# A projection by seven half-size products in place of eight, with its buffers in one ring, in a two-layer graph attention kernel on one Trainium2 core

## The chip, the core and the metric

The kernel runs on one core of a Trainium2 chip. The core has four compute engines with an instruction queue each: TensorE multiplies 128x128 blocks into PSUM, VectorE and ScalarE work elementwise on SBUF and PSUM, GpSimd does elementwise work and the indexed DMAs. SyncE issues most of the other DMAs. An instruction waits, on its engine, until what it needs is there; everything behind it on that engine waits too.

The metric is the time of one execution on the device, in microseconds, lower is better. In the profile PE is TensorE's multiplying, PEld its loading of weights, DVE is VectorE, ACT ScalarE, POOL GpSimd, SP SyncE. "L762" is line 762 of the kernel before.

## What is computed

The input is x, 16 batches of 1024 nodes with 256 features in float32, and one adjacency matrix of 1024 x 1024. Two layers follow each other, each with a layer norm ahead and x added behind:

```python
def _gat(inp, adj_mask, W, a):
    h = jnp.matmul(inp, W)
    F_ = h.shape[-1]
    f1 = jnp.matmul(h, a[:F_, 0])
    f2 = jnp.matmul(h, a[F_:, 0])
    e = jax.nn.leaky_relu(f1[:, :, None] + f2[:, None, :], ALPHA)
    if adj_mask is not None:
        e = jnp.where(adj_mask[None, :, :] > 0, e, NEG_INF)
    att = jax.nn.softmax(e, axis=2)
    h_prime = jnp.einsum('bij,bjf->bif', att, h)
    return jax.nn.elu(h_prime)

def _L0_gnn_ref(x, adj, mlp1_w, mlp1_b, mlp2_w, mlp2_b, W_fc, a_fc, W_hand, a_hand):
    out = jax.nn.relu(jnp.matmul(x, mlp1_w) + mlp1_b)          # 256 -> 512
    residual = out
    out = _gat(jax.nn.relu(out), None, W_fc, a_fc)             # first attention, no mask
    out = jax.nn.elu(out) + residual
    out = jax.nn.relu(jnp.matmul(out, mlp2_w) + mlp2_b)        # 512 -> 256
    residual = out
    out = _gat(jax.nn.relu(out), adj, W_hand, a_hand)          # masked attention a
    out = jax.nn.elu(out) + residual
    return jax.nn.relu(out)

h = jnp.maximum(_layernorm(x, axis=-1), 0.0)
x = x + _L0_gnn_ref(h, adj, ...)
h = jnp.maximum(_layernorm(x, axis=-1), 0.0)
x = x + _L1_gnn_ref(h, adj, L1_gnn_W, L1_gnn_a)                # masked attention b
```

The change is about `h = inp · W_fc` of the first, unmasked attention: 1024 x 512 times 512 x 512 in each of the 16 batches.

## The kernel before

**Stages of one batch.** Layer norm and a transpose; `mlp1` (L748) writes `resT`, 128 partitions x 4 chunks x 1024 nodes (features on the partitions). `project` (L762) multiplies `resT` by `wfc_sb`: for each of 8 tiles of 128 nodes and each of two column halves g, four chunks of 128 features are added up in PSUM. A half has 257 columns; the last one is f1 (half 0) or f2 (half 1), since the weights carry the products with the attention vector. ScalarE copies each half (L764) into `h_nat`, and GpSimd takes f1 out and puts ones in its place (L766, L767).

**The unmasked attention has no products of 1024 x 1024.** Since its weights depend on f1 + f2 alone, the nodes are sorted by f2, prefix sums of the sorted rows are written as tables, and each node gathers two rows. The steps: `columns` and `send` lay out f2 as a row, `rank` (L808 to L815) counts on VectorE how many nodes stand ahead, `scatter` (L822) writes the rows of `h_nat` to memory in sorted order, `read_sorted` (L866) loads them into `xs`, `sum_before` and `sum_behind` (L894 to L909) form sums into `tt` and `xs`, `write_table` and `carry` write the tables `fine` and `coarse`, `gather` (L934) fetches rows of them into `got`, `share` (L946 to L949) forms the denominators, `mean` (L956, L959) the mean rows, and `merge` (L1006 to L1017) transposes them, applies elu and adds the residual in `resT`. For the first batch half of this is done by products instead.

**Then** `mlp2` (L1024), the projection of the masked attention a (L614), its weights on VectorE (L667) and products (L677), `finish`, `combine` and `update` (L689 to L710), the second layer norm, and the same for the masked attention b (L717 to L723).

**Order.** All of it is written out by hand. `at(name, lo, hi, steps)` gives each step a planned time, to which the table `SHIFT` adds a number; all steps are sorted by that time, and every engine has its instructions in that order. GpSimd's instructions are also chained to each other. A period of the plan is 142 units (134.15 us in the trace between two like bursts), and a batch's work is spread over several periods: the rows of batch b + 2 are projected, ranked and scattered in the period in which batch b is in the masked attentions, and the prefix sums and gathers of batch b + 1 lie between. The planned places of the projection:

```python
for t in range(NT):
    at("dense_rows1", t0 + BETWEEN[t], t0 + BETWEEN[t], [partial(dense[b].project, t, 1)])
...
at("dense_begin5", t0 - 33, t0 - 30.5, [partial(d.project, t, 0) for t in range(2)])
at("dense_begin6", t0 - 21, t0 - 8, [partial(d.project, t, 0) for t in range(2, NT)])
```

**Buffers.** Each tag is a ring: an allocation takes the next buffer of the tag, and its first writer waits for the last reader of what was there. `seq` has two full-size buffers, which `h_nat`, `xs`, `tt` and `got` take in turn; `hm` has two of half that size for the projected rows of the masked attentions; `att` has eight of 128 x 256 for the masked weights.

Of the kernel before, what the change touches and what calls it, by code (L numbers as in the profile page):

```python
# [17 lines left out]
P = 128  # L18
HALF = 512
# [9 lines left out]
D_MIN = 1.0e-7  # L29
SHIFT = {  # L30
    "end dense_begin1": (-2.54,),
    "end dense_begin2": (-0.99,),
    "end dense_begin4": (9.79, 10.84, 0, 0, 0, -3.05, 0, -5.96,),
    "end dense_begin5": (-23.89, -15.67,),
    "end dense_begin6": (-20.81, 0, -12.64, -10.02, -11.47, -12.26,),
    "end dense_begin7": (-3.07,),
    "end dense_end1": (-7.17, -1.95,),
    "end dense_end2": (-6.38, -6.38, -6.38, -6.38,),
    "end dense_rows1": (-10.51, -6.24, -6.82, 0, 0, 0, 0, -4.24,),
    "end dense_sums1": (-48.96,),  # L40
    "end dense_sums10": (-21.95,),
    "end dense_sums2": (8.53, 0, 0, 3.76, -8.53, -12.13, -7.88, -5.24,),
    "end dense_sums3": (-9.59, -12.4,),
    "end dense_sums4": (-7.91, -7.91, -7.91, -7.91, -3.45, -3.45, -3.45, -3.45,),
    "end dense_sums6": (10.61,),
    "end dense_sums7": (-3.22, -4.43, -3.58, -3.26, 0, -0.77, 0, 4.02,),
    "end dense_sums8": (3.76,),
    "end dense_sums9": (2.37,),
    "end early_gathers2": (10.03, 10.03,),
    "end early_gathers3": (-5.29, 18.84, 14.56, 18.48,),  # L50
    "end early_gathers4": (0, 0.45, 0, 0, 10.2, 15.36, 8.86, 10.63,),
    "end first_mlp1": (-7.09, 0, 0, -10.32,),
    "end first_mlp2": (-4.41, -4.41, -4.41, -4.41,),
    "end masked_first1": (-9.1,),
    "end masked_first10": (0, 0.7, -4.33, -3.67, -2.03, -1.81, -3.41,),
    "end masked_first11": (0, 0, -4.93, -4.17, -2.96, -1.43, -4.36, -0.47,),
    "end masked_first12": (0, -1.5,),
    "end masked_first13": (0, 0, -4.74, -4.15, 0, 0.69, 1.51, 0.6,),
    "end masked_first14": (0.61, 3.4, -2.77, -2.71, 0.32, 3.65, 1.3, 0.83,),
    "end masked_first15": (-2.98,),  # L60
    "end masked_first16": (0.15,),
    "end masked_first2": (-8.7,),
    "end masked_first4": (-7.99,),
    "end masked_first5": (-9.93, -3.59, -1.25,),
    "end masked_first7": (-18.06, 0, 3.52, 24.98,),
    "end masked_first9": (-2.7, -2.7, -2.7, -2.7, -2.7, -2.7, -2.7, -2.7, -1.13, -0.9, -1.12,
        -1.51, -1.92, -2.78, -3.21, -3.56, -4.22, -2.23, -1.85, -1.53, -1.76, -2.17, -2.28, -2.05,
        -5.73, -5.67, -4.93, -4.1, -4.46, -4.69, -5.08, -4.71, -7.38, -5.64, -6.02, -5.94, -4.67,
        -3.38, -2.99,),
    "end masked_second1": (0, 0, 0, 0, 0, 0, -2.7, -2.7, -2.7, -2.7, -2.7, -2.7, -4.75, -4.45, 0,  # L70
        0, 0, 0, 0, 1.61, 1.54, 3.47, 3.07, 3.3, -3.32, -2.79, 0, 0, 0, 0.67, -6.09, -6.45, -6.84,
        -3.49, 0, 2.45,),
    "end masked_second2": (0, 0, 0, 0, 0, 0, 3.2, 2.96, 0.23, 0.23, 0, 2.22,),
    "end masked_second3": (-0.67, -0.43, 0, 0, -0.54, 3.58, 2.58, 1.28,),
    "end masked_second4": (0, 0, 0, 0, 0, 2.18, 2.56, 4.8,),
    "end masked_second5": (14.49, 8.09, 12.75, 21.36, 24.19, 12.45,),
    "end masked_second6": (0, 17.47,),
    "end merges1": (-2.65, -5.36, -2.83, -5.06, 0, 2.68, 2.67, 0.66,),
    "end merges2": (-2.65, -5.24, 5.1, 1.49, 3.05, 1.93, 4.16, 11.78,),
    "end scatters1": (8.25, 10.06, -7.13, -3.44, -5.23, -10.63, 0, -8.12,),  # L80
    "end second_mlp1": (1.82, 4.66, 8.88, 11.17,),
    "end second_mlp2": (-9.26, -9.26, -9.26, -9.26, -9.26, -9.26, -9.26, -9.26,),
    "end second_mlp3": (-9.24,),
    "end second_norm1": (-4.45, -1.81, -4.63, -4.57, -4.39, -5.31, -5.93, -6.31,),
    "end second_norm2": (-6.82,),
    "end second_norm3": (-6.84,),
    "end second_norm4": (-7.95,),
    "end second_norm5": (-8.56, -3.63, -2.16, -3.25, -3.33, -6.23, -7.8,),
    "end second_norm6": (-7.46,),
    "end second_norm8": (0, 0, 0, 0, 31.85,),  # L90
    "end turn_at1": (-3.4, 0, 0, -4.89, -0.78, -0.78, -0.78, -0.78,),
    "end turn_at2": (0, 0, 0, 0.78, -1.37, -1.37, -1.37, -1.37,),
    "end weights a": (-5.34, -5.34, -5.34, -5.34, -5.34, -5.34, -5.34, -5.34, -1.3, -1.76, -8.73,
        -6.94, -1.68, -8.23, 0, 1, 0.15, 0, 0, 0, -7.3, 1.55, 0, 0, -2.46, -12.74, -3.66, -1.38,
        -1.88, -1.72, -2.61, -5.89, -4.74, -29.97, -2.33, -12.21, -4.28, -4.33, -3.77, -7.66,),
    "end weights b": (-7.6, -7.02, -8.62, -8.6, -3.43, -3.15, -2.16, 1.28, -7.9, -5.17, -3.12,
        1.84, 1.74, 2.72, -12.96, -7.11, -4.91, -8.89, -1.88, -2.69, -5.62, -3.89, -12.92, 1.63,
# [1759 lines left out]
```

## Time and profile before

| what | value |
|---|---|
| time, median of 3 runs | 2252.36 us (2252.07 to 2253.29) |
| the profiled execution's own time | 2251.37 us |
| its span in the profile | 2249.6 us |
| PE busy | 2207.2 us, 98% of the span |
| DVE busy | 1643.1 us, 73% |
| ACT busy | 1259.6 us, 56% |
| POOL busy | 954.4 us, 42% |
| moved by DMA | 368.95 MB, 164 GB/s in the mean |

The span runs from the first to the last instruction; the execution's time has 1.8 us more. A group's row of the profile has the line, the engine, the operation, what it writes and reads, shapes and type, the count, then busy time, the mean length of one, and the idle time of the engine just ahead of them with what ended it. Lengths of PE rows overlap: the sum of their rows may exceed PE's busy time. A wait's row has who waited for whom, the sum, the count and the longest.

### The profile page before, as it was taken

To read this page: it belongs to the slowest core of one execution; us is meant where nothing else is said; L and a number is where in the kernel's file an instruction comes from. 1 tells how busy PE (TensorE), PEld (TensorE's weight loads), DVE (VectorE), ACT (ScalarE), POOL (GpSimd) and SP (SyncE) were. 2 spreads that over 40 slices of the span, in tenths; PEclk is the share of its full clock that TensorE was granted. 3 is DMA by queue.
4 is the path that set the end of the run, shared out by engine and by line. 5 is a ranking of instruction groups with operands and counts; after the bars stand their busy time and mean duration, and the time that the engine had idled before them with its cause. 6 is when DMAs were issued, how large, how long until landed. Compare 5 with 4: busy or idle time off the path is not lost.

```text
span 2249.6 us, 31025 instructions
## 1 busy us (share of the span) xinstructions
PE 2207.2 (98%) x9754; PEld 1723.4 (77%) x9754; DVE 1643.1 (73%) x4535; ACT 1259.6 (56%) x2797; POOL 954.4 (42%) x1212
## 2 busy tenths in 40 slices
PE   7999999999999999999999999999999999999997
PEld 5767777787877878787787877878787787877776
DVE  7677676777867678776776867677786776858765
ACT  5355745547365564756557375564746557365542
POOL 1163425263452536425263452636435263543620
PEclk9999999999999999999999999999999999999999
DMA  5568466675766757566685666757566585645700
GB/s 197 159 175 196 114 208 154 186 183 148 197 123 200 187 168 190 137 196 148 192 191 147 189 127 194 188 177 189 130 205 144 185 197 153 164 125 169 178 22 28
DMA packets 263870, 368.95 MB, mean 164 GB/s; under 512 B 124352, under 2 KB 175880, under 8 KB 259600
## 3 DMA queue, kind: packets, MB, share of 16 engines
q1 hardware_dynamic: 217088, 202.72, 31.9%
q0 software_dynamic: 45952, 163.99, 28.9%
q8 instruction: 80, 1.31, 0.3%
q14 instruction: 94, 0.77, 0.1%
q10 hardware_dynamic: 656, 0.17, 0.0%
HBM read 226.88 MB, written 126.29 MB: 157 GB/s over the span
## 4 chain that ended last, share of the span: by engine, by line
PE 75%; DVE 6%; DMA 2%; POOL 2%; ACT 1%; issue 1%; POOLq 0%; DVEq 0%; ACTq 0%; SPq 0%
PE oa L677 17%; PE h L762 16%; PE ob L677 14%; PE m L1024 8%; PE m L748 6%; PE pa L614 4%; PE pb L614 3%; PE hpT L1006 2%; DMA got<-coarse,k 2%; DVE attb L667 1%; PE carry L918 1%; PE on L1038 1%; PE nt L536 1%; DVE stats L516 1%; DVE hp L959 1%
## 5 line engine op out<-in xcount | busy, mean ns | idle before, releaser
L677 PE MATMUL ob<-hmb,attb 128*128 128x257 f32 x2048 | 463.9, 380 | 2.2 <-DVE attb L667 1.9
L762 PE MATMUL h<-wfc_sb,resT 128*128 128x257 f32 x2048 | 462.8, 379 | 0.0
L677 PE MATMUL oa<-hma,atta 128*128 128x258 f32 x2048 | 459.9, 382 | 1.8 <-DVE atta L667 1.5
L677 PEld LDWEIGHTS ob<-hmb,attb 128*128 128x128 f32 x2048 | 383.9, 190 | 67.2 <-issue 12.3
L677 PEld LDWEIGHTS oa<-hma,atta 128*128 128x128 f32 x2048 | 384.8, 190 | 59.3 <-DVE atta L667 2.9
L762 PEld LDWEIGHTS h<-wfc_sb,resT 128*128 128x128 f32 x2048 | 380.1, 189 | 59.1 <-issue 7.4
L705 POOL TENSOR_TENSOR posa<-posa,onat 128x256 f32<-128x256 f32 x118 | 106.7, 904 | 546.1 <-ACT posa L693 487.6
L667 DVE SCALAR_TENSOR_TENSOR attb<-rowsb,qwdb,edge 128x256 f32<-128x256 f32 (+1 forms) x536 | 292.1, 563 | 34.6 <-PE ob L677 28.6
L667 DVE SCALAR_TENSOR_TENSOR atta<-rowsa,qwda,edge 128x256 f32<-128x256 f32 (+1 forms) x520 | 257.3, 524 | 51.4 <-DMA rowsa<-row_a 35.6
L934 POOL DMA_INDIRECT got<-coarse,k x124 | 203.4, 1640 | 90.9 <-DMA got<-fine,k 56.6
L748 PE MATMUL m<-hT,w_sb 128*128 128x512 f32 x512 | 236.6, 596 | 1.9 <-ACT rb L719 1.1
L1024 PE MATMUL m<-resT,w_sb 128*128 128x512 f32 x512 | 228.3, 593 | 1.0 <-POOL resT L1017 1.0
L719 ACT ACTIVATE rb<-ob,recb 128x256 f32<-128x256 f32 x128 | 58.5, 474 | 274.9 <-DVE recb L717 248.9
L1017 POOL TENSOR_TENSOR resT<-resT,e 128x512 f32<-128x512 f32 x128 | 165.5, 1295 | 104.9 <-DVE e L1016 96.7
L692 ACT ACTIVATE ea<-oa,reca 128x256 f32<-128x256 f32 x128 | 60.3, 471 | 248.1 <-DVE reca L689 228.7
L934 POOL DMA_INDIRECT got<-fine,k x124 | 126.7, 1022 | 128.5 <-DVE hpd L999 41.9
L1024 PEld LDWEIGHTS m<-resT,w_sb 128*128 128x128 f32 x512 | 94.5, 190 | 102.4 <-issue 93.5
L748 PEld LDWEIGHTS m<-hT,w_sb 128*128 128x128 f32 x512 | 94.2, 191 | 89.0 <-issue 74.7
L822 POOL DMA_INDIRECT sorted<-hnat,place x128 | 128.6, 1004 | 53.9 <-DVE place L815 33.0
L764 ACT COPY hnat<-h 128x257 f32<-128x257 f32 x256 | 90.8, 367 | 104.1 <-PE h L762 101.6
L845 ACT ACTIVATE junk<-r,fs 128x1024 int8<-128x1024 f32 x124 | 142.6, 1150 | 0.9 <-POOL fs L766 0.6
L1016 DVE SCALAR_TENSOR_TENSOR e<-hpT,e 128x512 f32<-128x512 f32 x128 | 87.9, 688 | 53.2 <-ACT e L1010 53.0
(195 smaller groups left out, 3391.2 us busy)
## 6 DMA issues: line engine op xcount, KB each, us to landing
xs<-sorted SPq DMA_DIRECT2D x32, 1028.0 KB
fine<-tt SPq DMA_DIRECT2D x32, 1026.0 KB
fine<-xs SPq DMA_DIRECT2D x32, 1026.0 KB
x<-in_x_dram SPq DMA_DIRECT2D x16, 1024.0 KB
xn<-in_x_dram SPq DMA_DIRECT2D x15, 1024.0 KB
out_dram<-x SPq DMA_DIRECT2D x28, 512.0 KB
hT<-xn SPq DMA_DIRECT2D x416, 32.0 KB
coarse<-carry SPq DMA_DIRECT2D x32, 256.5 KB
```

The costliest lines, as they stand in the source:

```text
L614: nc.tensor.matmul(ps[:, :2 + F], lhsT=hT[:, c, t * P:(t + 1) * P], rhs=self.w_sb[:, c, 0, :], start=(c == 0), stop=(c == FC - 1))
L667: nc.vector.scalar_tensor_tensor(a_t[:, :n * P], self.rows[:, i], self.qwd[:, 1, j:j + 1], edge[:, j, i], op0=OP.max, op1=OP.mult)
L677: nc.tensor.matmul(self.out[t][:, :F + self.ONES], lhsT=self.att[t0, j][:, (t - t0) * P:(t - t0 + 1) * P], rhs=self.hm[:, j, 2:2 + F + sel ...
L705: adder.tensor_add(pos, pos, o_nat[:, t, :])
L748: nc.tensor.matmul(ps, lhsT=w1_sb[:, kc, c * P:(c + 1) * P], rhs=piece(kc, h), start=(kc == 0), stop=(kc == FC - 1))
L762: nc.tensor.matmul(ps[:, :F + 1], lhsT=self.resT[:, kc, t * P:(t + 1) * P], rhs=wfc_sb[:, kc, g, :], start=(kc == 0), stop=(kc == HC - 1))
L764: nc.scalar.copy(self.h_nat[:, t, g, :], ps[:, :F + 1])
L822: made = nc.gpsimd.indirect_dma_start(out=sorted_d[self.b % 2], out_offset=bass.IndirectOffsetOnAxis(ap=self.place[:, t:t + 1], axis=0), i ...
L845: nc.scalar.activation(junk, self.r2, AF.Sign, bias=self.fs[:, 0, t:t + 1], accum_out=self.signs[:, t:t + 1])
L934: nc.gpsimd.indirect_dma_start(out=got[u // n][:, u % n, :], out_offset=None, in_=(coarse_d if coarse else fine_d)[self.b % 2][:, :], in_o ...
L1017: nc.gpsimd.tensor_add(dst, dst, e)
L1024: nc.tensor.matmul(ps, lhsT=w2_sb[:, kc, c * P:(c + 1) * P], rhs=self.resT[:, kc, h * HALF:(h + 1) * HALF], start=(kc == 0), stop=(kc == H ...
```

## The change

**The projection.** `resT` is cut in 2 x 2 blocks (upper and lower 512 nodes; first and last two chunks of features), and so is the weight (chunks by column halves g). Seven products by the scheme of Strassen and Winograd give the four blocks of h. For each pair u of node tiles (u and u + 4) the products 1, 6, 5 and 3 add up in one PSUM bank, and after each of them ScalarE copies the running sum out as one of the four blocks; product 7 of two pairs goes to another PSUM buffer and VectorE adds it to two blocks (`add_pair`); products 2 and 4 are separate and are added by VectorE to the blocks that hold f1. A product has two chunks of 128 features.

**The sums.** Each pair needs four sums of blocks of `resT`, two on VectorE and two on GpSimd (`sums_of`). Four sums of weight blocks are formed once, on GpSimd (`seven_weights`). The weight block that is overwritten there is first stored to memory, and read from there in each batch (`load_b21`, two DMAs of 128 x 257).

**Buffers.** `seq` and `hm` become one ring of six half-size buffers: `h_nat`, `xs` and `tt` take two each, `got` four of two tiles, the two masked projections one each. The sums and the re-read weight block take buffers of the ring `att`, which are widened to 257 columns. Some small tiles move to other tags or have fewer buffers. `share` works on pairs of tiles.

**The places.** The steps of the sort, the scatter and the prefix sums have new planned times, `send` of the masked attention b is placed by the next batch's period, the start is rearranged, and the whole table `SHIFT` is new.

```diff
+SEQ = 6
 SHIFT = {
...
-        a_bc = big.tile([P, 2, fo], F32, tag="seq" if parts == 2 else "hm", name=name + "_a",
-                        bufs=2)
+        a_bc = big.tile([P, 2, fo], F32, tag="seq", name=name + "_a", bufs=SEQ)
...
+    def seven_weights():
+        top, low = slice(0, 2), slice(2, HC)
+        b11, b12, b21, b22 = [wfc_sb[:, k, g, :] for k in (top, low) for g in range(2)]
+        nc.sync.dma_start(wfc_d.rearrange("p (k f) -> p k f", k=2), b21)
+        nc.gpsimd.tensor_sub(wfc_more[:, 1], b22, b12)
+        nc.gpsimd.tensor_sub(b12, b12, b11)
+        nc.gpsimd.tensor_sub(wfc_more[:, 0], b22, b12)
+        nc.gpsimd.tensor_sub(b21, b21, wfc_more[:, 0])
...
+    def att_tile(name):
+        return big.tile([P, F + 1], F32, tag="att", name=name, bufs=ATT)
...
-        def project(self, t, g):
...
-            ps = mm_psum(f"h_{self.b}_{t}_{g}")
-            for kc in range(HC):
-                nc.tensor.matmul(ps[:, :F + 1], lhsT=self.resT[:, kc, t * P:(t + 1) * P],
-                                 rhs=wfc_sb[:, kc, g, :], start=(kc == 0), stop=(kc == HC - 1))
-            nc.scalar.copy(self.h_nat[:, t, g, :], ps[:, :F + 1])
-            if g == 0:
-                nc.gpsimd.tensor_copy(self.fs[:, 0, t:t + 1], self.h_nat[:, t, 0, F:])
-                nc.gpsimd.memset(self.h_nat[:, t, 0, F:], 1.0)
+        def sums_of(self, u, which):
...
+            if which == 1:
+                nc.vector.tensor_add(t, a21, a22)
+            elif which == 2:
+                nc.vector.tensor_sub(t, self.s[1, u], a11)
+            elif which == 3:
+                nc.gpsimd.tensor_sub(t, a11, a21)
+            else:
+                nc.gpsimd.tensor_sub(t, a12, self.s[2, u])
+
+        def load_b21(self):
+            self.b21 = [att_tile(f"b21_{self.b}_{k}") for k in range(2)]
+            for k in range(2):
+                nc.sync.dma_start(self.b21[k], wfc_d[:, k * (F + 1):(k + 1) * (F + 1)])
+
+        def multiply(self, ps, lhs, rhs, start):
+            for k in range(2):
+                nc.tensor.matmul(ps, lhsT=lhs[:, k, :], rhs=rhs[k], start=start and k == 0,
+                                 stop=k == 1, skip_group_check=True)
+
+        def step(self, i, u):
...
+            if i in (1, 6, 5, 3):
+                if i == 1:
+                    self.chain[u] = mm_psum(f"h_{self.b}_{u}")
+                ps = self.chain[u][:, :F + 1]
+                self.multiply(ps, a, b, i == 1)
+                t, g = {1: (u, 0), 6: (u + TH, 0), 5: (u + TH, 1), 3: (u, 1)}[i]
+                nc.scalar.copy(self.rows_of(t)[:, g, :], ps)
+            elif i == 7:
+                if u % 2 == 0:
+                    self.pair = bc_psum(f"h7_{self.b}_{u}")
+                self.multiply(self.pair[:, u % 2 * HALF:u % 2 * HALF + F + 1], a, b, True)
+            else:
+                ps = mm_psum(f"h{i}_{self.b}_{u}")[:, :F + 1]
+                self.multiply(ps, a, b, True)
+                t = u if i == 2 else u + TH
+                h = self.rows_of(t)[:, 0, :]
+                nc.vector.tensor_add(h, h, ps)
+                nc.gpsimd.tensor_copy(self.fs[:, 0, t:t + 1], h[:, F:])
+                nc.gpsimd.memset(h[:, F:], 1.0)
+
+        def add_pair(self, u):
+            ps = self.pair.rearrange("p (u f) -> p u f", u=2)[:, :, :F + 1]
+            for g in (1, 0):
+                dst = self.h_nat[u // 2][:, 2:4, g, :]
+                nc.vector.tensor_add(dst, dst, ps)
+
+        def rows_of(self, t):
+            h, u = divmod(t, TH)
+            k, v = divmod(u, 2)
+            if k not in self.h_nat:
+                self.h_nat[k] = big.tile([P, TH, 2, F + 1], F32, tag="seq",
+                                         name=f"hnat_{self.b}_{k}", bufs=SEQ)
+            return self.h_nat[k][:, 2 * h + v]
...
     def dense_rows(t0, b):
 
-        for t in range(NT):
-            at("dense_rows1", t0 + BETWEEN[t], t0 + BETWEEN[t], [partial(dense[b].project, t, 1)])
+        d = dense[b]
...
+            at("dense_rows1", t0 + lo, t0 + lo, [partial(d.sums_of, u, i)])
+        for lo, i, u in ((85.3, 1, 0), (86.2, 1, 1), (87.1, 7, 0), (88, 7, 1), (89.2, 6, 0),
+                         (90.2, 6, 1), (91.2, 1, 2), (92.2, 1, 3), (93.4, 5, 0), (94.4, 5, 1),
+                         (95.6, 3, 0), (96.6, 3, 1), (98, 7, 2), (99, 7, 3), (100, 6, 2),
+                         (101, 6, 3), (103.6, 5, 2), (104.6, 5, 3), (107, 3, 2), (108, 3, 3)):
+            at("dense_rows2", t0 + lo, t0 + lo, [partial(d.step, i, u)])
+        for lo, u in ((96, 0), (106, 2)):
+            at("dense_rows3", t0 + lo, t0 + lo, [partial(d.add_pair, u)])
+        at("dense_rows4", t0 + 107.5, t0 + 107.5, [d.load_b21])
...
-        at("dense_begin1", t0 - 38.5, t0 - 38.5, [d.columns])
-        at("dense_begin2", t0 - 36.8, t0 - 36.8, [d.send, partial(d.row, True)])
-        at("dense_begin3", t0 - 31.5, t0 - 31.5, [d.highest])
-        at("dense_begin4", t0 - 28, t0 - 12, each(d.rank, range(NT)))
-        at("dense_begin5", t0 - 33, t0 - 30.5, [partial(d.project, t, 0) for t in range(2)])
-        at("dense_begin6", t0 - 21, t0 - 8, [partial(d.project, t, 0) for t in range(2, NT)])
-        scatters(d, t0 - 18.5, t0 - 4.5)
-        at("dense_begin7", t0 - 6, t0 - 6, [d.query])
-        at("dense_begin8", t0 - 4, t0 - 4, [d.read_sorted])
+        at("dense_begin1", t0 - 32.8, t0 - 32.8, [d.columns])
+        at("dense_begin2", t0 - 31.5, t0 - 31.5, [d.send, partial(d.row, True)])
+        at("dense_begin3", t0 - 27, t0 - 27, [d.highest])
+        at("dense_begin4", t0 - 24, t0 - 8, each(d.rank, range(NT)))
+        late = late_steps(d)
+        at("dense_begin5", t0 - 31, t0 - 28, late[:2])
+        at("dense_begin6", t0 - 22, t0 - 10, late[2:])
+        scatters(d, t0 - 16, t0 - 2)
+        at("dense_begin7", t0 - 4, t0 - 4, [d.query])
+        at("dense_begin8", t0 - 1.5, t0 - 1.5, [d.read_sorted])
...
-        at("dense_sums1", t0 - 3, t0 - 3, [d.sums_begin])
+        at("dense_sums1", t0 - 1, t0 - 1, [d.sums_begin])
...
-            at("second_norm7", lo + 24, lo + 24, [m.send])
+            at("second_norm7", base_of(b + 1) - 44.7, base_of(b + 1) - 44.7, [m.send])
```

`late_steps` are the products 2 and 4 of the four pairs.

## The prediction

> **What bounds the kernel now.** I read the busy shares first, then the chain of waits, then one period of the steady state as a window, then the waits of the engine that came out of it.
>
> The page's busy times, and its shares of the chain that ended last, by engine:
>
> ```profile
> PE 2207.2 (98%) x9754; PEld 1723.4 (77%) x9754; DVE 1643.1 (73%) x4535; ACT 1259.6 (56%) x2797; POOL 954.4 (42%) x1212
> ...
> PE 75%; DVE 6%; DMA 2%; POOL 2%; ACT 1%; issue 1%; POOLq 0%; DVEq 0%; ACTq 0%; SPq 0%
> ```
>
> TensorE is busy 98% of the span: 2249.6 − 2207.2 = 42.4 us idle in all. "Busy" can hide slack, so I took three batch periods, cut where the same projection burst recurs (columns: interval, its length, then busy time of PE, PEld, DVE, ACT, POOL, the granted clock, DMA share, GB/s):
>
> ```profile
> 781.43:915.58 134.15, 134.15 (x591) 105.20 (x591) 100.56 (x272) 77.76 (x175) 60.76 (x77) 1.00 0.65 173
> 915.58:1051.16 135.58, 134.65 (x592) 105.18 (x591) 99.42 (x272) 77.64 (x175) 61.46 (x77) 1.00 0.65 171
> 1051.16:1185.39 134.23, 134.23 (x591) 105.13 (x591) 99.41 (x272) 78.03 (x176) 61.66 (x77) 1.00 0.66 173
> ```
>
> TensorE has no gap in two of the three periods and 0.9 us in the third, at full clock; VectorE has 34 us spare in each. The waits of the engines say the same: TensorE's largest is the first layer norm, once; its others are a few us in all.
>
> ```profile
> PE nt L536 <- POOL rstd L522: 11.1, 1, 11.1
> ...
> PE hpT L1006 <- DVE hp L959: 2.0, 4, 0.7
> ```
>
> So a period is a sum of TensorE instructions, and removing some shortens it, as long as nothing else needs more than the new sum.
>
> **What the change removes.** The rows it removes and nearly adds:
>
> ```profile
> L762 PE MATMUL h<-wfc_sb,resT 128*128 128x257 f32 x2048 | 462.8, 379 | 0.0
> L764 ACT COPY hnat<-h 128x257 f32<-128x257 f32 x256 | 90.8, 367 | 104.1 <-PE h L762 101.6
> L723 DVE TENSOR_TENSOR x<-x,rb 128x256 f32<-128x256 f32 x128 | 52.1, 424 | 11.7 <-ACT rb L719 11.7
> L1008 DVE TENSOR_SCALAR e<-hpT 128x512 f32<-128x512 f32 x128 | 84.9, 682 | 54.8 <-PE hpT L1006 49.6 <-POOL resT L1017 2.9 <-PE line_ps L496 1.2
> L705 POOL TENSOR_TENSOR posa<-posa,onat 128x256 f32<-128x256 f32 x118 | 106.7, 904 | 546.1 <-ACT posa L693 487.6
> ```
>
> The projection is 64 fp32 products of 128x257 a batch; the trace has each as two instructions, 64 × 16 × 2 = 2048. The mean of 379 ns overlaps its neighbours, so it isn't the price. The chain of waits gives the pitch, in two places alike (start, length, instructions):
>
> ```profile
> 781.43 6.94 PE h L762 x32
> ...
> 915.58 6.94 PE h L762 x32
> ```
>
> 6.94 / 32 = 216.9 ns an instruction. Seven products × 4 row-tile pairs × 2 chunks = 56 a batch replace the 64: 8 × 16 × 2 = 256 instructions fewer, × 0.2169 = **55.5 us**, or 3.47 a period. Groups are two chunks long instead of four; L748 has groups of two and L1024 of four at the same mean (596 and 593 ns), so I price the shorter groups at nothing.
>
> **What it adds, by engine, over 16 batches.**
>
> - **ScalarE:** 16 copies of 128x257 a batch before and after: nothing.
> - **VectorE:** 128 sums of 128x256 at L723's 424 ns = 54.3. Products 2 and 4 are added from PSUM, 128 × 257 wide; no such row, so between L723's 0.424 and L1008's 0.682 for twice the width: 0.45, 58. The pair add, 64 × 514 wide, at L1008's 0.69 = 44. Four more small ones a batch in the shares, at the 0.165 of L946 to L949, 10. Sum +166: 1643 → 1809. In a period 99.8 → 110.2 of a new length of 134.2 − 3.5 = 130.7: 84%. Beside TensorE's work, so nothing on the path; if the cover goes, rival B.
> - **GpSimd:** 128 subtractions at L705's 904 ns, +116: 954 → 1070, half of the span. Hidden; they have no one behind them but the scatters and gathers of the same queue.
> - **SP and DMA:** two 131 KB loads of one weight block a batch, 4.2 MB to 369 MB moved: 1%, issued some 15 us ahead of product 2. Nothing. The queue isn't tight: SP's issues take 0.2 to 0.8 us.
> - **Buffers:** one ring of six halves holds what two rings held. A half now comes free when its own last reader is done, but waits for the ring's order: the first copy into h_nat must wait until half 0's gathered rows are read by the mean. On ScalarE other copies are queued behind that copy, and TensorE's chain step behind them. In TensorE's order the mean is far ahead of it; I take nothing, and 0.5 us a period as the other end.
>
> [...] VectorE adds and GpSimd subtracts now run side by side on SBUF. In the timeline before (start, length):
>
> ```profile
> 1076.38 1.27 POOL L1017 TENSOR_TENSOR resT<-resT,e 128x512 f32<-128x512 f32 x1
> ...
> 1076.61 1.19 DVE L812 SCALAR_TENSOR_TENSOR junk<-r,fs,after 128x128 uint8<-128x128 f32 x1
> ```
>
> L812's median is 352 ns; beside a GpSimd addition it took 1190. [...] By the rows, the weights of L667, with two SBUF inputs, average 582 ns against a median of 479, so 0.1 us over all their collisions: the new work would bring 20 to 30. I take the rows. [...]
>
> **New waits in the product chain.** Products 1, 6, 5, 3 add up in one PSUM bank, and ScalarE copies the running sum after each, so a step on the same bank waits for that copy. By the new order of TensorE's instructions at least two other products of 4 × 0.217 = 0.87 us lie between, 1.7 us against a copy of 0.37. If a copy stands behind a long ScalarE instruction (L845, 1.15) it is 1.5: just covered. The columns and the rank row wait for product 2's and the pair's adds; some 6 us of TensorE lie between. Behind a waiting step everything on TensorE is queued. Bounds: nothing, and 20 steps a batch by one late copy in twenty of 1 us, 1 us a period; I take 0.3 × 14 steady periods = **4 us**.
>
> **Moved places.** Columns, ranks, scatters, the sorted read and the prefix sums come 1.5 to 5.7 planned units (142 to a period) later against the gathers, which stay. In TensorE's order, at before's durations, the stretch from columns to the first mean is 112 us before and 105.3 after: 6.7 us less for a chain that waits for DMA and VectorE. It has slack: the mean's shares wait for the gathered rows (100.1 us over 28 times) and TensorE feels 0.7 at most.
>
> ```profile
> DVE den L946 <- DMA got<-coarse,k: 100.1, 28, 8.0
> ```
>
> I cost it at nothing and keep 6.7 as the other end (rival C).
>
> **The start.** The weight block is stored to memory, subtracted by GpSimd, and the store stands on SP behind the zero rows, whose last issue is at 31.19 us. The first sums wait behind it on GpSimd. Bounds 0 and 5 us (four 128x514 subtractions there at L1017's 1.3 us, none covered); I take half, **2.5**, since TensorE has other products of the first layer to do meanwhile.
>
> **The sum.** Profiled run 2251.37 (span 2249.6 and 1.8 around it) − 55.5 + 2.5 + 4 = 2202.4. The median of the runs lies 1.0 above the profiled one: **2203 us**.
>
> **The rivals.**
>
> - **A, TensorE keeps the end:** 2203, 0.65. For it: no gap in three periods. Its own range is 2194 to 2212, from chain waits of 0 to 1 us a period and the start's bounds.
> - **B, VectorE's queue shows through:** chain steps, sums or masked weights come 1 to 2 us late a period because VectorE runs at 84% and is locked in places. In the rank stage it is full already (10.00 of 10.00 us from 1110 to 1120). Against it: from 1160 to 1170 it is busy for 2.02 of 10, so lateness is made up within a period. 14 × 1.2 to 2 = 17 to 28 on the forecast: about 2225, 0.2.
> - **C, the other side:** the sort, sums and gather chain becomes the period. It loses 6.7 us of cover; once its slack is used, each period is the chain's. All of it late: 6.7 − 3.47 = +3.2 a period, 14 × 3.2 = 45: 2252 + 45 = about 2297. It decides from 3.5 us of lateness a period. For it: waits of up to 8.0 us for gathered rows; against it: those sit on VectorE, and TensorE's wait behind them is 0.7. 0.12.
> - **D, the seven products aren't shorter:** a bank switch or a group of two costs 27 ns more an instruction (1792 × 0.027 = 48, the saving is gone): no change. L748's mean speaks against it. 0.03.
>
> Changes of less than 0.2%, 4.5 us, can't be told from none here. Faster 0.65 + 0.2 = 0.85, same 0.03, slower 0.12. The range holds A and most of B: 2191 to 2226.
>
> **What would show it.** The projection at 1792 instructions with a pitch of 217 ns; periods of 130.5 to 131 with TensorE as busy as they are long; VectorE near 1810, GpSimd near 1070. Under B TensorE's waits name the new adds or the copies; under C its waits name the mean, and the wait for gathered rows falls on every period. I am wrong if TensorE's idle time is well over 50 us.

## The result: faster by 0.7%, a third of what was forecast

| | kernel before | changed kernel |
|---|---|---|
| median of 9 runs | 2253.29 us | 2236.58 us |
| lowest and highest | 2249.35, 2255.99 | 2232.01, 2246.17 |
| ratio | 1 | 0.993, 95% interval 0.9914 to 0.9947 |
| profiled execution, its span | 2251.37, 2249.6 us | 2232.1, 2230.4 us |

The change saves 17 us in the medians, 19.3 in the profiled executions. The forecast was 2203, from 2191 to 2226: the direction was right, the time lies outside the range.

The changed kernel's busy times, from its page:

```profile
PE 2172.5 (97%) x9498; PEld 1672.8 (75%) x9498; DVE 1776.0 (80%) x4929; ACT 1261.9 (57%) x2797; POOL 1067.5 (48%) x1344
```

256 matmul instructions are gone. GpSimd has gained what the forecast said (1070 forecast), VectorE less (133 us for 166). But TensorE's busy time fell by 34.7 us, not by 55.5, and its idle time rose from 42.4 to 57.9. Three periods, cut where the first vector of the masked attention a recurs (interval, length, busy time of PE, PEld, DVE, ACT, POOL, granted clock, DMA share, GB/s):

```profile
827.53:960.31 132.78, 131.57 (x576) 102.01 (x575) 107.88 (x297) 77.85 (x174) 67.96 (x86) 1.00 0.67 177
960.31:1093.21 132.90, 132.16 (x576) 101.86 (x575) 108.08 (x297) 77.78 (x174) 67.88 (x86) 1.00 0.67 177
1093.21:1225.37 132.16, 131.56 (x576) 102.01 (x575) 107.85 (x297) 77.85 (x174) 68.23 (x86) 1.00 0.66 178
```

The count is near what it should be, 576 for 591 where 16 fewer were forecast. The length is 132.2 to 132.9, where 134.2 − 3.5 = 130.7 was counted on, and each of the three has 0.6 to 1.2 us of idle time, where two of before's three had none. The rest of the 1.5 to 2.2 us isn't shown as idle: ends of matmuls are modelled in the trace, so a short gap can be counted as busy. For that reason I use starts of instructions from here on.

One product per batch, the first score vector of the masked attention a, marks the batches. First the kernel before, then the changed one (after the count: lengths, then first and last start):

```profile
L491 PE MATMUL extpsa<-ident,exta x16: 272/273/295, 170.8 to 2156.0; 128*128 128x128 f32 x16
```

```profile
L539 PE MATMUL extpsa<-ident,exta x16: 272/273/323, 182.5 to 2143.0; 128*128 128x128 f32 x16
```

That cuts the span in three. Two batches' saving (6.9 us) falls into the start, the other 14 (48.6) into the middle:

| stretch | before | without loss | changed | lost | forecast |
|---|---|---|---|---|---|
| start, to the first mark | 170.8 | 163.9 | 182.5 | 18.6 | 2.5 |
| middle, 15 intervals | 1985.2 | 1936.6 | 1960.5 | 23.9 | 4 |
| end, from the last mark | 93.6 | 93.6 | 87.4 | −6.2 | 0 |

TensorE's waits in the changed kernel, largest first (who waits for whom: us in all, times, longest):

```profile
PE nt L584 <- DVE hn L574: 10.2, 2, 9.9
PE m L1132 <- POOL resT L1125: 8.5, 3, 3.9
PE oa L725 <- ACT resT L801: 4.4, 7, 1.3
PE extpsb L539 <- DVE extb L670: 4.0, 2, 3.6
PE linea_ps L544 <- ACT qwda L687: 3.5, 10, 0.4
...
PE hpT L1114 <- DVE e L1124: 2.3, 4, 1.2
PE h L827 <- ACT hmb L664: 2.2, 5, 0.8
...
PE h L827 <- POOL s L816: 1.7, 2, 1.1
```

The first row is the first layer norm, as before. The second is the start: residual additions on GpSimd, for which `mlp2` of the first batch waits. In the fourth, 3.6 us are a single wait near the end, at 2092 us. The others are new or larger than before, most of them recur with the batches, and they aren't the waits of one resource: a product of the masked attention waits for ScalarE, a score vector for ScalarE, the new products for a copy on ScalarE and for differences on GpSimd, a transpose for VectorE. By the starts of the instructions (each distance to the next start less the usual one of its shape, summed by what comes next, the middle against before's and divided by 14), a period loses about 0.6 us ahead of the new products, 0.4 ahead of `oa`, 0.4 ahead of the score vector's line and 0.2 ahead of the transposes.

Two of them in the timeline of the changed kernel (start, length, engine and line, what, idle before and its releaser). The score vector:

```profile
960.31 0.27 PE L539 MATMUL extpsa<-ident,exta 128*128 128x128 f32 x1
960.42 1.03 PE L725 MATMUL ob<-hmb,attb 128*128 128x257 f32 x4
...
961.80 0.27 PE L544 MATMUL linea_ps<-ident,qwda 128*8 128x128 f32 x1 [0.35 <-ACT qwda L687]
```

The vector goes from TensorE through VectorE and ScalarE back to TensorE, and only four matmul instructions of 257 columns, 0.87 us, lie between its two visits; in before four of 512 columns stood there, 1.72 us (from 959.87 to 961.59). And the masked attention:

```profile
838.94 0.30 ACT L996 ACTIVATE bd<-xs,topd 128x4 f32<-128x4 f32 x1 [1.85 <-DMA xs<-sorted]
...
839.34 0.67 ACT L801 ACTIVATE resT<-m,b_sb 128x512 f32<-128x512 f32 x1
...
840.06 0.70 PE L725 MATMUL oa<-hma,atta 128*128 128x258 f32 x2 [0.80 <-ACT resT L801]
```

ScalarE stands 1.85 us at a small instruction that needs the sorted rows from memory; behind it stands the activation that empties a PSUM bank of `mlp1`, and TensorE's `oa` stands at that bank until 0.05 us after the activation's end. ScalarE is 57% busy and waited for all the same, because an instruction that waits holds up those behind it in its queue.

### The profile page after: what moved, and what is told of

Same layout as the page of the kernel before. It is cut to its first block, busy times and chain, and to the rows that moved or that the text cites. A ratio compares the mean times of both kernels' runs of the same rounds, so it can differ in the third digit from the quotient of the medians.

```text
span 2230.4 us, 31158 instructions
## 1 busy us (share of the span) xinstructions
PE 2172.5 (97%) x9498; PEld 1672.8 (75%) x9498; DVE 1776.0 (80%) x4929; ACT 1261.9 (57%) x2797; POOL 1067.5 (48%) x1344
## 5 line engine op out<-in xcount | busy, mean ns | idle before, releaser
L725 PE MATMUL ob<-hmb,attb 128*128 128x257 f32 x2048 | 473.3, 381 | 0.4 <-DVE attb L715 0.2
L715 DVE SCALAR_TENSOR_TENSOR atta<-rowsa,qwda,edge 128x256 f32<-128x256 f32 (+1 forms) x520 | 239.8, 494 | 71.8 <-DMA rowsa<-row_a 67.6
L753 POOL TENSOR_TENSOR posa<-posa,onat 128x256 f32<-128x256 f32 x118 | 98.5, 835 | 384.3 <-ACT posa L741 383.6
L715 DVE SCALAR_TENSOR_TENSOR attb<-rowsb,qwdb,edge 128x256 f32<-128x256 f32 (+1 forms) x536 | 268.0, 528 | 8.2 <-PE ob L725 4.1
L801 ACT ACTIVATE resT<-m,b_sb 128x512 f32<-128x512 f32 x128 | 87.4, 685 | 159.8 <-PE m L798 159.8
L754 POOL TENSOR_TENSOR ea<-ea,posa 128x256 f32<-128x256 f32 x118 | 99.1, 839 | 90.4 <-ACT ea L747 59.5
L767 ACT ACTIVATE rb<-ob,recb 128x256 f32<-128x256 f32 x128 | 57.9, 474 | 146.0 <-DVE recb L765 136.2
L1068 DVE SCALAR_TENSOR_TENSOR hp<-got,den,part 128x513 f32<-128x513 f32 x120 | 103.9, 878 | 38.6 <-ACT part L1065 36.9
L1117 ACT ACTIVATE e<-e 128x512 f32<-128x512 f32 x128 | 79.9, 624 | 95.7 <-DVE e L1116 94.5
```

Of the source, the lines that this page charges most:

```text
L715: nc.vector.scalar_tensor_tensor(a_t[:, :n * P], self.rows[:, i], self.qwd[:, 1, j:j + 1], edge[:, j, i], op0=OP.max, op1=OP.mult)
L725: nc.tensor.matmul(self.out[t][:, :F + self.ONES], lhsT=self.att[t0, j][:, (t - t0) * P:(t - t0 + 1) * P], rhs=self.hm[:, j, 2:2 + F + sel ...
L753: adder.tensor_add(pos, pos, o_nat[:, t, :])
L754: adder.tensor_add(e, e, pos)
L801: nc.scalar.activation(self.resT[:, c, h * HALF:(h + 1) * HALF], ps, AF.Relu, bias=b1_sb[:, c:c + 1])
L1068: nc.vector.scalar_tensor_tensor(hp, got[:, K:], den[:, 0, u:u + 1], part, op0=OP.mult, op1=OP.add)
```

## The experiments

Ratios are to the kernel before on the same chip (2250 us in these series), with 95% intervals. The question for all of them: are the lost 23.9 us of the middle due to what was added (sums, adds, copies, ring, new places), or to the taking away itself?

### Take the products out, add nothing

To the kernel before, leaving out one chunk of four in column half 1, so 256 instructions:

```diff
-            for kc in range(HC):
+            chunks = HC - g
+            for kc in range(chunks):
```

> The kernel before, without the fourth feature chunk of the products of column half 1: 8 of 64 products of a batch less, as many as the change saves, and nothing added or moved (half 1 of h then lacks a quarter of its sum). If the old order can turn the removed 55 us of TensorE's work into time, 2253 - 55 = about 2198 and periods near 130.7. If the sort and gather chain bounds a period once TensorE is shorter, the saving is cut to about what the change showed: 2225 to 2240, with TensorE's new waits behind rows read back from memory.

Measured 2223.36 us, ratio 0.9877 (0.9861 to 0.9894): 27 of 55 us. With no new work, no new buffer and no moved step, half of the saving is lost. Its waits on TensorE, largest first:

```profile
PE hpT L1007 <- DVE hp L960: 12.4, 20, 1.4
PE hpT L1007 <- DVE e L1017: 12.3, 15, 1.8
```

These were 2.0 and 1.5 us in before. The removed products stood between the transposes of the merges, and covered the time in which VectorE makes the next mean rows. With eight fewer, the transposes come earlier than their rows. The chain that ended last, followed back from the last instruction at each step to what released it, has changed too; its shares of the span by engine:

```profile
PE 58%; DVE 11%; DMA 6%; POOL 5%; ACT 3%; issue 3%; ACTq 0%; DVEq 0%; POOLq 0%; SPq 0%
```

In before TensorE had 75%. Followed through a middle period, the chain now leaves TensorE for some 45 us (1131.7 to 1177.0): it runs over the second layer norm on VectorE, the gathers on GpSimd behind it, the landing of their rows, and the mean rows of a merge.

### The same number of products out of another place

Also to the kernel before, one of the eight node chunks of the masked attention b left out in each tile:

```diff
         def product(self, t0, n, j):
+            if self.which == "b" and j == 3:
+                return
```

> The kernel before with as many products of TensorE left out as the change saves, 8 of 257 columns a batch, but out of the middle of masked attention b (one of its eight node chunks isn't added there) and not out of the projection. If the projection's products were worth little because they stood as cover between the merges' transposes, products that stand elsewhere are worth nearly their full 55 us: 2250 - 55 = 2195 to 2205. If the sort and gather chain or another engine holds every period, it is 2220 or more, as with the projection's own.

Measured 2223.56 us, 0.9888 (0.9872 to 0.9905). The expectation fell: this place is no better. The largest wait, one instance of it, and ScalarE at the place:

```profile
PE m L750 <- ACT rb L721: 14.9, 11, 1.7
```

```profile
1009.97 1.98 PE L750 MATMUL m<-hT,w_sb 128*128 128x512 f32 x4 [1.31 <-ACT rb L721]
```

```profile
1009.44 0.47 ACT L721 ACTIVATE rb<-ob,recb 128x256 f32<-128x256 f32 x1 [5.33 <-DVE recb L719]
```

One place a period, some 1.4 us, where a PSUM bank is released behind the finishing of attention b on ScalarE. ScalarE itself waits there for VectorE, 5.33 us, in which VectorE works without a pause through masked weights, updates and the next layer norm. So the loss isn't in the merges as such. At both places tried, TensorE's hand-overs through VectorE and ScalarE have little to spare, and of 3.5 us of products taken out the next hand-over takes back about half.

The marks of the two kernels, this one second:

```profile
L491 PE MATMUL extpsa<-ident,exta x16: 272/273/295, 165.4 to 2130.2; 128*128 128x128 f32 x16
```

```profile
L491 PE MATMUL extpsa<-ident,exta x16: 272/273/295, 171.8 to 2131.0; 128*128 128x128 f32 x16
```

The middle of the first is 1964.8 us where 1936.6 would be without loss: 28.2 lost. The middle of the second, in which 234 of the removed instructions lie, is 1959.2 for 1934.4: 24.8 lost. The change lost 23.9. So the taking away alone is enough for a loss of this size in the middle. Where the changed kernel is worse than the first of these two is the start: its first mark comes 17.1 us later, its middle is 4.3 shorter and its end 5.6.

### Is it the gathered rows?

The merges of the first experiment wait for rows that come by gathers, so I left out the gathers of coarse rows from batch 2 on, nearly half of all gathers, in that kernel and in the changed one:

```diff
         def gather(self, h, coarse, u):
+            if coarse and self.b >= 2:
+                return
```

> The kernel before with an eighth of its projection's products left out, and also without the gathers from the coarse table from batch 2 on. Alone, the products left out gave 27 of 55 us. If the gather chain had the rest, TensorE's waits ahead of the merges' transposes (25 us) go and the time comes to 2253 - 55 = about 2198 to 2202. If something else holds the period, it stays near 2223.

> The changed kernel without the gathers from the coarse table from batch 2 on (the second of the two rows that each node adds up is left out there): half of the gathers' bytes and 13 us of GpSimd's time a period go, nothing on TensorE, VectorE or ScalarE. If the chain from the sort over tables and gathers to the merges is what a period waits for, periods fall from 133.0 to TensorE's own 130.3 plus the local 1 us of the score line and attention a's first product: about 131.2, so 2236 - 14 x 1.6 = about 2213. If TensorE's small waits come from VectorE's load or single places alone, under 5 us: 2232 or more.

With the products only taken out: 2216.76 us, 0.985 (0.9834 to 0.9867), 6.6 less than without this edit (the intervals overlap a little) and far from the forecast. The merges' waits stay:

```profile
PE hpT L1009 <- DVE e L1019: 11.6, 16, 1.8
...
PE hpT L1009 <- DVE hp L962: 7.7, 14, 0.7
```

The chain that ended last has no DMA left to speak of:

```profile
PE 70%; DVE 7%; ACT 5%; issue 3%; POOL 1%; DMA 0%; ACTq 0%; DVEq 0%; POOLq 0%; SPq 0%
```

So the gathers are not all that the transposes are late for: without them the same transposes wait behind work that passes between ScalarE and VectorE in the merges, and ten of the fifteen intervals between marks stand at 132.4 us, where 130.7 was forecast. In the changed kernel: 2219.41 us, 0.9863 (0.9846 to 0.9879), some 15 better than the change; its middle is 1943.4 us, 17.1 shorter, the most that any run gave back of the 23.9, while its first mark comes 6.0 later. The `h` waits for copies are gone, those at `linea_ps` (3.0 us, 9 times) and `oa` (2.3, 5 times) are not. So in the changed order the late rows are a large part: the copies of `hmb` stand on ScalarE behind the scaling of gathered rows. The edit also frees GpSimd and the DMA queues of those gathers, so not all of this need be the one wait.

### Take one added cost away at a time

From the changed kernel. Without the 16 block sums of a batch, the products taking the blocks themselves:

```diff
-            if which == 1:
-                nc.vector.tensor_add(t, a21, a22)
...
+            self.s[which, u] = {1: a21, 2: a22, 3: a11, 4: a12}[which]
```

> The changed kernel without its 16 block sums a batch (products 3, 5, 6, 7 read blocks of the transposed rows directly, so h is another one): 128 sums less on VectorE, about 54 us, and 128 subtractions less on GpSimd, about 110 us. If the added load is what TensorE waits for, most of the 2 us a period go, and some of the start: about 2200. If it is the order of a few steps, and transfers that ScalarE waits for ahead of copies out of PSUM, the periods stay at 132 to 133 and the time within 10 us of 2236.

Measured 2221.55 us, 0.9867 (0.9851 to 0.9884), about 14 better than the change; its middle is 1949.9 us, 10.6 shorter. Without VectorE's adds of products 2, 4 and 7:

```diff
-                nc.vector.tensor_add(h, h, ps)
...
-                nc.vector.tensor_add(dst, dst, ps)
```

> The changed kernel without VectorE's additions of products 2, 4 and 7 to the blocks (h lacks them): 192 instructions, about 100 us of VectorE, and the columns no longer wait for them. If VectorE's fuller queue makes TensorE late, more than the block sums' 14 us go: 2215 or less. If it is places and cover, under 8 us: 2228 to 2236.

Measured 2228.77 us, 0.9911 (0.9894 to 0.9927): VectorE falls to 1698 us of work, the time by some 4 us, and the intervals of this kernel and of the change overlap. So VectorE's load as such is not the main cause. The sums do more; they are on GpSimd as well, hold `att` buffers, and stand ahead of the products, but which of these counts isn't separated.

### Move steps at the places that wait

Score vectors of attention a 2.3 units sooner, five steps of the prefix sums 0.2 to 2 units later, so that the ScalarE instruction waiting for sorted rows stands behind the last copies of `mlp1`:

```diff
-        at("masked_first1", t0 + 1, t0 + 1, [m.vectors])
+        lo = t0 + 1 - 2.3 * (2 <= b < NB - 3)
+        at("masked_first1", lo, lo, [m.vectors])
...
-    "mid dense_sums3": (-4.26,),
-    "mid dense_sums4": (-5.2, -5.2, -5.2, -5.2, 0.28, -0.96, -2.208, -3.2,),
+    "mid dense_sums3": (-2.3,),
+    "mid dense_sums4": (-3.2, -3.85, -4.4, -4.95, 0.28, -0.96, -2.208, -3.2,),
```

> The changed kernel with two steps moved for batches 2 to 12 or all middle batches: the score vectors of masked attention a 2.3 units sooner, and ScalarE's weights for the prefix sums behind the last copy of the first layer's product instead of ahead of it (the sums behind them 1 to 2 units later). If the lost time sits in single places of the order, the 0.5 us before the score line and the 0.6 before the first product of attention a go in some 11 periods: 8 to 12 us less, about 2226. If the lateness comes from the load, it turns up at other places and the time stays within 3 us of 2236.

Measured 2229.01 us, 0.9911 (0.9894 to 0.9927), overlapping the change's interval. In its trace the waits at `linea_ps` and `oa` are gone, and the `h` waits in the middle have grown from 8.2 to 14.3 us by the starts: most of the gain is lost again at the next place.

### The start

Three kernels, each the changed one with one edit: the weight block's store from ScalarE's queue, the first batch's gathers issued in a row on GpSimd ahead of the merges' additions, and eight spare products in the two waits of `mlp2` so that TensorE isn't idle there.

```diff
-        nc.sync.dma_start(wfc_d.rearrange("p (k f) -> p k f", k=2), b21)
+        nc.scalar.dma_start(wfc_d.rearrange("p (k f) -> p k f", k=2), b21)
```

> The changed kernel with the one store of the weight block issued from ScalarE's queue, not from SP's behind eight writes of zero rows. If that store holds the first batch's last block sums and so the whole first sort, the first batch's columns come 3 to 7 us sooner, the two long waits of TensorE near 145 and 150 us shrink, the halved clock from 157 us may go: 5 to 12 us less, 2225 to 2232. If VectorE's and GpSimd's fuller queues make the start late, nothing: 2236.

```diff
-    "start gathers1": (0, 0, 0, 9,),
-    "start gathers2": (5.8, 5.8, 5.8, 5.8,),
+    "start gathers1": (0, 0, 0, 0,),
+    "start gathers2": (-0.4, -0.8, -1.2, -1.6,),
```

> The changed kernel with one move: the first batch's gathers stand on GpSimd in one row ahead of the merges' additions and the small copies, not between them. If GpSimd's order makes the two waits of 3.9 and 3.1 us near 145 and 150 us, both shrink below 2 us, the clock isn't halved there, and 8 to 15 us go: 2221 to 2228. If the first batch's sort is late for other reasons, under 3 us: about 2235.

```diff
+                if (self.b, h, c) == (0, 0, 0) and kc < 2:
+                    spare = tr_psum(f"spare_{kc}")
+                    for i in range(4):
+                        nc.tensor.matmul(spare, lhsT=ident, rhs=w1_sb[:, 0, :HALF],
+                                         start=True, stop=True)
```

> The changed kernel with eight spare products of 128x512, read by nobody, in the two waits near 145 and 150 us of the start, four in each; 3.4 us of TensorE's work each, less than the wait. If the idle time brings the half clock that follows, the 10.2 us at half speed from 157 us go and up to 5 us with them: about 2231. If the clock is halved for another reason, or nothing waits for TensorE there, it stays at 2236 or rises by up to 1.

The store does nothing: 2236.01 us, 0.9936 (0.9919 to 0.9952). The term that the forecast had priced, SP's queue, isn't the loss. The order on GpSimd is part of it: 2225.09 us, 0.9892 (0.9875 to 0.9908), 9 better and with an interval apart from the change's. GpSimd and TensorE of the changed kernel at the place:

```profile
145.07 1.58 POOL L1044 DMA_INDIRECT got<-coarse,k  x1 [0.60 <-issue]
...
146.09 1.85 POOL L1125 TENSOR_TENSOR resT<-resT,e 128x512 f32<-128x512 f32 x1
...
147.99 2.08 PE L1132 MATMUL m<-resT,w_sb 128*128 128x512 f32 x2 [3.87 <-POOL resT L1125]
...
153.17 7.20 PE L1132 MATMUL m<-resT,w_sb 128*128 128x512 f32 x12 [3.10 <-POOL resT L1125]
```

Gathers and residual additions alternate on GpSimd, and `mlp2` waits for one addition after the other; with the gathers issued first, the two waits are 2.09 and 1.52 us. A caution: of the 9 us the profiled execution shows only 2 at the first mark (180.8) and the rest in the middle, whose scatter from one profiled execution to another is some 3.5 us either way: four kernels with the same order there, the change and these three, took 1960.5, 1961.2, 1954.0 and 1957.1. The median tells the size, not the place.

### Both moves together

> The changed kernel with the moved steps of the run on places and the mended row of gathers of the run on the start, together. The two act on different stretches (middle periods, first 180 us): if each loss is its own, 5 + 9 = 14 us less than the change, 2221 at 2236 of the change. If the lateness is one chain that runs through all batches, one of the two gains is lost: 2226 or more.

Measured 2222.61 us, 0.9873 (0.9856 to 0.9889), 12 to 13 below the change. Within the intervals the two gains add up (4 and 9); it isn't clear of noise that this kernel beats the one with the start alone (2225.09). Then, on top of it, the two last copies of `hmb` ahead of the scaling of gathered rows:

```diff
-    "mid second_norm1": (-5.2, 0, 0, -4.1, 4.1, 0, 0, 1.6,),
+    "mid second_norm1": (-5.2, 0, 0, -4.1, 4.0, 0, 0, 1.4,),
```

> The kernel with both gains, and in the middle periods the last two tiles of the projection of masked attention b 0.1 to 0.2 units sooner: their copies out of PSUM then stand on ScalarE ahead of the first scaled rows of the mean, which wait there for gathered rows. If the wait of about 1 us a period near the projection's first chains is ScalarE standing behind those gathered rows, it falls below 0.4 and 6 to 10 us go: 2213 to 2217. If TensorE then waits at the next place for the same rows (the merges' transposes), under 3 us: 2220 or more.

Measured 2222.01 us, 0.9871 (0.9855 to 0.9888): nothing. In its waits the place has a new name:

```profile
PE h L827 <- ACT hnat L849: 5.3, 13, 0.7
```

The copy of `hmb` isn't waited for any more; the next copy in ScalarE's queue is, behind the same scaling.

## Why the forecast was right in direction and wrong in size

**The work removed: right.** 256 instructions × 216.9 ns = 55.5 us was forecast, 256 fewer ran, and the new products are not dearer than the old ones. Four of them in a row take 0.87 us from the first start to the next instruction's (142.23 to 143.10), 0.217 each, and the median distance from one start to the next is 216 to 217 ns for each kind of them, 216 in before. The rows by shape (count, busy, mean ns):

```profile
L827 PE MATMUL h<-wfc_sb,resT 128*128 128x257 f32 x512 | 128.1, 381 | 2.2 <-ACT hmb L664 2.2
...
L827 PE MATMUL h<-wfc_more,s 128*128 128x257 f32 x512 | 126.1, 382 | 1.9 <-POOL s L816 1.7
...
L827 PE MATMUL h<-wfc_sb,s 128*128 128x257 f32 x512 | 125.0, 381 | 0.7 <-ACT hnat L849 0.6
...
L827 PE MATMUL h<-b,resT 128*128 128x257 f32 x256 | 63.6, 380 | 0.0
```

These are 1792 instructions. With the pitch as it was, rival D is refuted; the means (381 ns against 379) overlap as before.

**The work added: right in size, not in who waits for it.** Adds from PSUM took 0.42 us in the mean (0.45 forecast), pair adds 0.68 (0.69), VectorE's block sums 0.45 and 0.47 (0.424), GpSimd's subtractions 0.74 and 0.86 (0.904). VectorE works for 107.9 us of a period of 132.6, GpSimd for 68. Of GpSimd's subtractions the forecast said that "they have no one behind them but the scatters and gathers"; but products 7 and 3 read them, and TensorE waited for L816.

**The step that failed** is the one ahead of the sum: "So a period is a sum of TensorE instructions, and removing some shortens it, as long as nothing else needs more than the new sum." The proviso was tested on busy times of a whole period, in which VectorE had 34 us to spare. But a period holds dozens of hand-overs from TensorE through VectorE, ScalarE or memory and back, each covered only by the products that stand between. That no gap was seen in two periods says that each cover is long enough; it doesn't say by how much. (The other waits, "a few us in all", were 2.4 us from 300 to 1900 us, but 20 over the whole span.) The two kernels that only take products out of before's order measure it: 27 us of 55 are saved, at two different places. So half of the saving was lost without any of the change's additions, in the middle as much as the change lost there, and none of the terms of the sum stood for it.

**"0.3 × 14 = 4" for waits in the product chain, "I cost it at nothing" for moved places, "I take nothing" for the ring:** together 4 against 23.9 in the middle. The kinds of wait named were right in part. The forecast said of ScalarE's queue that copies stand behind one that waits, and "TensorE's chain step behind them"; that is what `h` waiting for `hmb` is. It blamed the ring of buffers; what ScalarE waits for in the traces is gathered and sorted rows. The moved places let the sorted rows be late for `bd` and put the score vectors where only four short products cover them: some 4 us by the ratios, if the overlapping intervals hold it.

**The start, 2.5 against 18.6.** The bounds were 0 and 5, from the store and the subtractions behind it; giving the store another queue gained nothing. "The start is rearranged" was read in the diff but never priced: the order on GpSimd is worth 9 us. The rest isn't settled. In the trace the first batch's columns come 7 us later than before (55.3 for 48.3) and the read of its sorted rows 18 us later (92.4 for 74.0); why, no run tells.

**The end** was forecast as unchanged and is 6.2 us shorter. No run asked why. A slip of the sum besides: from the bounds that the forecast names, 0 to 14 us for the chain and 0 to 5 for the start, rival A's own range is 2197 to 2216, not 2194 to 2212.

**The rivals.** B forecast 2225 for VectorE's queue. Its time was nearer than the forecast's; its mechanism is only partly there: less load on VectorE gives 4 us, and TensorE waits more for ScalarE than for VectorE's new adds, though with products left out of before's order it is VectorE's queue that ScalarE waits for at the second place. C, slower by 45, is refuted in its sign and size: but the wait that it named, gathered rows, does reach TensorE, through ScalarE, and is worth up to 15 us in the changed kernel. Behind B's "locked in places" the trace of before has this: the 14 instructions of L812 that overlap a GpSimd addition (L1017) took 1.18 us in the median, the other 114 took 0.35. The forecast's estimate of such overlaps, from the rows of L667, was 20 to 30 us of VectorE's time (its 582 ns are attention b's weights alone, attention a's average 528), outside its sum of 1809; VectorE's busy time came to 1776.

What stays open: what the additions cost in the middle of the changed kernel. The taking away alone loses as much in before's order (28.2 and 24.8 for 23.9), but these can't simply be subtracted, since places and orders differ: in the changed order, leaving out the sums gives 10.6 back and leaving out gathers 17.1, and each repair of a place moved waits rather than ended them.

## What to carry to other kernels

In an order written out by hand, products on the busiest engine are also the cover of the hand-overs between them: price a removal by the slack of the next hand-over, not by the sum of instructions. That slack can be measured before the change is written, by leaving as many instructions out of the old kernel; had it been done here, it would have said 27 us and not 55, and left only the start, where the change lost 18.6, to be found. Where waits then appear at many places with different names, one repair moves the wait to the next place, and an engine that is 57% busy can be the one waited for, when an instruction that waits for memory stands ahead in its queue.

## What the runs showed of the hardware

TensorE ran at half clock in the start of the changed kernel. In before, whose last product ends at 2239.30 us, the trace's record of the clock has it at half only from 2242.26 on. Windows in the start, first the changed kernel, then the one with spare products in the two waits (columns as above):

```profile
140.00:150.00 10.00, 4.92 (x15) 2.10 (x13) 8.79 (x22) 7.73 (x13) 8.14 (x14) 0.83 0.73 138
150.00:160.00 10.00, 6.90 (x13) 2.82 (x12) 4.08 (x8) 4.08 (x7) 8.57 (x10) 0.66 0.87 206
```

```profile
140.00:150.00 10.00, 7.64 (x26) 4.10 (x26) 9.51 (x24) 8.35 (x14) 8.07 (x16) 1.00 0.65 130
150.00:160.00 10.00, 9.56 (x22) 3.56 (x20) 2.64 (x7) 3.49 (x7) 8.57 (x10) 1.00 0.92 212
```

A granted clock of 0.83 and 0.66 is 3.4 and 6.8 us at half, 10.2 in all, around idle times of 3.87 and 3.10 us. In the trace's record of the clock it lasts from 146.54 to 156.78 us, 10.24 us (157 us in the expectations is its end). Another half-clock stretch, of 3.413 us, begins at 2092.13, and a last one at 2228.67, when the last product, which ends at 2224.79, is done. The first is three times as long as the second, and the second begins 1945.60 us after it, 570 times 3.413. In the 3.41 us ahead of 146.54 TensorE was busy for 1.00, in the 3.41 us ahead of 2092.13 for none. What brings the half clock, the runs don't settle.

Two `mlp2` products took 2.08 us at half clock, and 1.02 shortly before. Yet in the profiled execution with the spare products, at a clock of 1.00 there, the first mark comes at 183.3 us, no sooner than the change's 182.5: behind these products TensorE waits for the next gathered rows, and reaches them sooner for nothing. The median is 2232.38 us, ratio 0.993 (0.9909 to 0.9951), as the change itself. Of the four executions two had a mean clock of 0.999 and took 2229 us, the others 0.997 and 0.996 and took 2239 and 2235: the spare products don't keep the clock full in every execution, and what it costs in those no trace tells. In the profiled one the slow clock, like an idle engine, would have cost only what a later wait took anyway.
